# Recurrence levels: only the second blocks' columns, two sets of PSUM banks, and ScalarE copies at the two widest levels

## The chip, the cores and the metric

The kernel runs on one core of one Trainium2 chip. The metric is device time in microseconds (us) of one execution. The engines of the core work side by side, each through its own queue in order: TensorE (matrix products, in the profile PE, with the weight loads apart as PEld), VectorE (DVE), ScalarE (ACT), GpSimd (POOL) and SyncE (SP, which issues transfers). TensorE writes its products to PSUM, and VectorE and ScalarE read them from there; GpSimd works on SBUF alone in this kernel.

## What is computed

The reference is a stack of eight steps on `x` of shape (2, 1024, 256) in float32: an adapter and a recurrent attention, a two-layer net and a mixture of experts, a sparse attention and a local attention, an adapter and a gated feed-forward net. The change lies in the recurrent attention, whose core is this scan over 1024 tokens for each of two sequences and four heads of 64 channels:

```python
def step(S, inputs):
    rt, kt, vt, wt = inputs
    kv = kt[..., :, None] * vt[..., None, :]
    y = jnp.einsum('bhi,bhij->bhj', rt, S + u[None, :, :, None] * kv)
    S = wt[..., :, None] * S + kv
    return (S, y)
```

Unrolled, token t gets from an earlier token s the value v[s], weighted by the sum over channels i of r[t,i] k[s,i] times the decays w[.,i] of all tokens between s and t; and from itself v[t], weighted with u in place of decays. The weights of all pairs (s, t) within a chunk of 128 tokens are what the kernel calls A; what comes from earlier chunks goes through a state of 64 x 64 for each head.

## The kernel before, in words

Channels lie on the 128 partitions, in two groups `c`: partition p of group c is channel 128c + p. A group holds two heads; `par` (0 or 1) says which, so `halves[par]` are the 64 partitions of one head. Tokens run along the free dimension: `r[b]`, `kk[b]` and `w[b]` are tiles of 128 x 2 x 1024 for sequence b. There are NC = 8 chunks of 128 tokens, each in two halves of H = 64 tokens. `A[b]` has the earlier token s on the partitions (two halves of 64) and, for each `par`, `c` and chunk, the later token t along the free dimension.

`wkv` (line 378) fills A by doubling. First the diagonal: `ru` is r times u (line 527, ScalarE), the products of k and ru of all pairs within each half chunk go to PSUM, and VectorE multiplies them with a repeated unit matrix into A (line 528). Then six levels, l = 0 to 5, with h = 2^l. At a level the tokens are seen as pairs of blocks of h tokens. The products of k and r of all pairs within each half chunk are formed again (`scores`, line 410), and of these only the pairs with s in the first and t in the second block of a pair of blocks are kept: VectorE's `copy_predicated` (line 537) copies, under a mask `k.lvl[:, l]`, the columns of the second blocks into A. After that `decay` (from line 420) multiplies k of all first blocks with the total decay of the second block (line 426, GpSimd), r of all second blocks with that of the first (line 427, VectorE), and forms the totals of the doubled blocks (line 429, VectorE). So k and r carry at each level just the decay between blocks that the level needs, and each level of a sequence needs the `decay` of the level before. `last` (line 432) does the step from 64 to 128: the products of each chunk's first half as s with its second half as t, copied to A by ScalarE and VectorE (line 446), with a last `decay`. The levels run for sequence 0 and sequence 1 in turn.

A step of a level has 2 groups x 8 chunks x 2 halves x 2 heads = 128 products. Each takes 64 x 64 weights (64 channels of one head, 64 tokens s) and 64 columns (tokens t). The head chooses the half of the array's rows, the half chunk that of its columns, so four different ones can lie in the array at once.

PSUM: `scores` and `last` use two tiles `sc0` and `sc1`, one per head, of 128 x (2 x 8 x 64) float32, 4 KB per partition each, in a pool with one buffer for each name. So all steps, of both sequences, use the same memory in turn, and the products of one step for a head wait until the copy of the step before has read that head's tile. Another pool (`wkq`, four banks) serves the state and output products.

What sets the order: the program is written as straight code, and the framework's planner places each instruction in its engine's queue by a priority that follows the program's order and by a model of when its operands are ready. It may take ready work ahead: the totals of line 429, which need the decays alone, stand before the levels in VectorE's queue (from 134.9 us), and in the timeline eight output products (line 498) stand at 211.9 us, among the last level's products. On each engine the queue then runs in order. Within a level the written order is: the products of sequence b, the copies of both heads, the multiply of k on GpSimd, the multiply of r on VectorE; then the other sequence.

After the last level, `states` transposes k (line 459), forms the chunk states (line 476) and scans them (line 486), and `output` forms y from A, v, the states and r (lines 498 and 509). The network's further steps follow from y.

Of the kernel before, what the change touches and what calls it, by code (L numbers as in the profile page):

```python
# [9 lines left out]
F32 = mybir.dt.float32  # L10
# [8 lines left out]
P = 128  # L19
# [43 lines left out]
def tiles(tc, **how):  # L63

    return tc.tile_pool(reuse_waits="tile", **how)
# [312 lines left out]
def wkv(k, r, kk, w, v, y, x):  # L378
# [6 lines left out]
    nc, tc = k.nc, k.tc  # L385
    NC = S // P
    M = NC - 1
    H = P // 2
    halves = [slice(i * H, i * H + H) for i in range(2)]
    with (  # L390
# [3 lines left out]
        eye = ap.tile([P, H], F32, name="eye")  # L394
# [3 lines left out]
        A = [ap.tile([P, 2, 2, NC, P], F32, name=f"A{b}") for b in range(B)]  # L398
# [1 line left out]
        for b in range(B):  # L400
            nc.gpsimd.memset(A[b][halves[1], :, :, :, H:P].rearrange("p a c n t -> p (a c n) t"), 0.0)

        def scores(pp, b, rr, take):
            ps = [pp.tile([P, 2, NC, H], F32, name=f"sc{par}") for par in range(2)]
            for c in range(2):
                for ck in range(NC):
                    for half in range(2):
                        ts = slice(ck * P + half * H, ck * P + (half + 1) * H)
                        for par in range(2):
                            nc.tensor.matmul(  # L410
                                ps[par][halves[half], c, ck, :],
                                lhsT=kk[b][halves[par], c, ts],
                                rhs=rr[halves[par], c, ts],
                                start=True,
                                stop=True,
                            )
            for par in range(2):
                take(A[b][:, par, :, :, 0:H].rearrange("p c n t -> p (c n) t"), ps[par].rearrange("p c n t -> p (c n) t"))

        def decay(sp, b, l):  # L420
            h = 1 << l
            n = 2 * S // (2 * h)
            t2 = tot[b].rearrange("p (n two) -> p n two", two=2)
            kv = kk[b].rearrange("p c (n two h) -> p (c n) two h", two=2, h=h)
            rv = r[b].rearrange("p c (n two h) -> p (c n) two h", two=2, h=h)
            nc.gpsimd.tensor_mul(kv[:, :, 0, :], kv[:, :, 0, :], t2[:, :, 1].unsqueeze(2).to_broadcast([P, n, h]))
            nc.vector.tensor_mul(rv[:, :, 1, :], rv[:, :, 1, :], t2[:, :, 0].unsqueeze(2).to_broadcast([P, n, h]))
            nt = sp.tile([P, n], F32, name=f"tot{l}", bufs=2)
            nc.vector.tensor_mul(nt, t2[:, :, 0], t2[:, :, 1])
            tot[b] = nt  # L430

        def last(pp, b):

            ps = [pp.tile([P, 2, NC, H], F32, name=f"sc{par}") for par in range(2)]
            for c in range(2):
                for ck in range(NC):
                    for par in range(2):
                        nc.tensor.matmul(
                            ps[par][halves[0], c, ck, :],
                            lhsT=kk[b][halves[par], c, ck * P : ck * P + H],  # L440
                            rhs=r[b][halves[par], c, ck * P + H : (ck + 1) * P],
                            start=True,
                            stop=True,
                        )
            for par, copy in enumerate((nc.scalar.copy, nc.vector.tensor_copy)):
                copy(
                    A[b][halves[0], par, :, :, H:P].rearrange("p c n t -> p (c n) t"),
                    ps[par][halves[0]].rearrange("p c n t -> p (c n) t"),
                )
            decay(ap, b, 6)  # L450

        def states(sp, b):
# [70 lines left out]
        with tiles(tc, name="wks", bufs=2) as sp, tiles(tc, name="wkp", bufs=1, space=PSUM) as pp:  # L523
            for b in range(B):
                ru = sp.tile([P, 2, S], F32, name="ru")
                for c in range(2):
                    nc.scalar.activation(ru[:, c, :], r[b][:, c, :], AF.Copy, scale=k.vec("u", c))
                scores(pp, b, ru, lambda d, ps: nc.vector.tensor_mul(d, ps, eye.unsqueeze(1).to_broadcast([P, 2 * NC, H])))
            for l in range(6):
                h = 1 << l  # L530
                for b in range(B):

                    def take(d, ps):

                        dv, pv = (t.rearrange("p g (n two h) -> p g n two h", two=2, h=h)[:, :, :, 1, :] for t in (d, ps))
                        m = k.lvl[:, l].rearrange("p g (n h) -> p g n h", h=h)
                        nc.vector.copy_predicated(dv, m, pv)

                    scores(pp, b, r[b], take)
                    decay(sp, b, l)  # L540
            for b in range(B):
                last(pp, b)
# [1160 lines left out]
def program(ctx: ExitStack, tc: tile.TileContext, ins, out):  # L1703
# [16 lines left out]
    with tiles(tc, name="w0", bufs=1) as wp:  # L1720
        load_adapter0(k, wp)
        with tiles(tc, name="rkwv", bufs=1) as ap:
            r, kk, w = ([ap.tile([P, 2, S], F32, name=f"{n}{b}") for b in range(B)] for n in "rkw")
            v = ap.tile([P, NBLK, C], F32, name="v")
            with tiles(tc, name="zero", bufs=1) as zp:
                load_attn0(k, wp, zp)
                load_late(k, lp)
                z = zp.tile([P, ROW], F32, name="z")
                nc.vector.memset(z, 0.0)
                for t, n in ((xs, 2 * NSLOT), (ys, 2 * T)):  # L1730
                    f = t.shape[-1]
                    for i in range(n // 1024):
                        nc.sync.dma_start(
                            out=t[i * 1024 : (i + 1) * 1024, :].rearrange("(p j) f -> p j f", p=P),
                            in_=z[:, 0:f].unsqueeze(1).to_broadcast([P, 8, f]),
                        )
                tmix_in(k, x, r, kk, w, v)
            with tiles(tc, name="y0", bufs=1) as yp:
                y = yp.tile([P, 2, T], F32, name="y")
                wkv(k, r, kk, w, v, y, x)  # L1740
# [139 lines left out]
```

## Time and profile before

| what | us |
|---|---|
| median of 3 runs (lowest, highest) | 1566.27 (1561.85, 1575.56) |
| profiled execution, its own time | 1573.28 |
| its span in the profile | 1571.6 |
| first diagonal product to first product of level 0 | 141.5 to 150.1 |
| the twelve level steps | 150.1 to 213.0 |
| last blocks' products | 213.0 to 222.6 |
| TensorE's products in the levels (1536), busy | 46.5 |
| VectorE's masked copies (24), busy | 20.3 |
| GpSimd's multiplies of k (14), busy | 32.2 |

Lines below such as `L410 PE MATMUL sc<-r,k 64*64 64x64 f32 x1536 | busy us, mean ns | idle` read: line of the program, engine, operation, tile written and tiles read, the part of the array used (rows*columns), partitions x elements, and the count; then the sum of their times, the mean of one, and the engine's idle time just before them with what ended it. In the timeline, a row begins with its start and the length of the merged stretch in us. In the table by stretches, each engine's busy time is followed by its count of instructions, then come the granted share of TensorE's full clock, the share of the transfer engines, and GB/s. TensorE's products are pipelined: a product's own duration contains its way through the array, and what it costs is the distance from start to start. "issue" is idle time that ended with no wait for another engine in the records.

### The profile page before, as it was taken

The numbers are of one execution on the slowest core, as the hardware profiler recorded it, in microseconds if no ns is written. First come the engines' busy times: TensorE is split into PE (matmuls) and PEld (weight loads), VectorE is DVE, ScalarE is ACT, GpSimd is POOL, SyncE is SP. The second block draws the span as 40 slices with busy tenths as digits, with TensorE's granted clock in tenths as the row PEclk, the third lists the DMA queues.
The fourth block names the chain that finished last, engine by engine and source line by source line (L and its number), as shares of the span: only waits on it lengthen the run. The fifth ranks groups of instructions, "written<-read, shape, count | busy, mean of one in ns | idle before, by whom it ended". The sixth has DMA issues, their size and how long they took to land. (4 is left out here: it accounts for less than half of the span.)

```text
span 1571.6 us, 27458 instructions
## 1 busy us (share of the span) xinstructions
PE 1453.8 (93%) x10842; PEld 994.2 (63%) x10842; DVE 876.0 (56%) x2791; ACT 686.1 (44%) x1675; POOL 186.6 (12%) x167
## 2 busy tenths in 40 slices
PE   5998779999869999979999989999999999999897
PEld 2445768544646676655666634778886478888765
DVE  3544663599931111055888711788782167878454
ACT  2433013333421212204988821667574265656543
POOL 1532430014411011010000010000000000000021
PEclk8899678999979999987999999999999999999999
DMA  9500003401153333030000020000000000000001
GB/s 301 176 1 2 3 3 112 161 4 40 53 162 132 124 115 115 14 120 1 2 2 2 2 82 0 1 2 2 1 2 1 0 1 2 2 1 2 1 19 36
DMA packets 42631, 70.79 MB, mean 45 GB/s; under 512 B 7040, under 2 KB 35712, under 8 KB 39424
## 3 DMA queue, kind: packets, MB, share of 16 engines
q1 hardware_dynamic: 36224, 56.11, 10.7%
q0 software_dynamic: 3072, 8.65, 1.5%
q10 hardware_dynamic: 3200, 4.19, 0.8%
q8 instruction: 88, 1.44, 0.4%
q14 instruction: 47, 0.39, 0.1%
HBM read 45.09 MB, written 23.86 MB: 44 GB/s over the span
## 5 line engine op out<-in xcount | busy, mean ns | idle before, releaser
L1543 ACT ACTIVATE pe<-pe,nm 128x320 f32<-128x320 f32 x256 | 141.9, 555 | 133.3 <-DVE nm L1533 133.1
L1533 DVE CUSTOM_DVE_ANT_0 pe<-ps,wbs 128x320 f32<-128x320 f32 x256 | 118.7, 487 | 5.9 <-PE ps L1527 2.5
L1174 ACT ACTIVATE pe<-pe,nm 128x256 f32<-128x256 f32 x256 | 110.6, 498 | 22.1 <-DVE nm L1164 22.1
L942 PE MATMUL ph<-xt,w 128*128 128x512 f32 x256 | 114.2, 604 | 2.0 <-ACT xt L937 2.0
L1523 PE MATMUL ps<-kT,qT 64*128 64x384 f32 (+1 forms) x512 | 109.2, 498 | 3.3 <-DVE qT L1497 2.8
L950 PE MATMUL po<-w,h 128*128 128x256 f32 x512 | 111.8, 379 | 0.0
L950 PEld LDWEIGHTS po<-w,h 128*128 128x128 f32 x512 | 97.3, 190 | 16.6 <-issue 3.8
L1164 DVE CUSTOM_DVE_ANT_0 pe<-ps,lc 128x256 f32<-128x256 f32 x256 | 94.0, 417 | 19.7 <-PE ps L1148 19.7
L953 DVE TENSOR_TENSOR ye<-po,b 128x256 f32<-128x256 f32 x32 | 13.6, 425 | 163.8 <-PE po L950 163.8
L881 DVE SCALAR_TENSOR_TENSOR lc<-iok,idx,lc 128x256 f32<-128x256 f32 x248 | 103.7, 476 | 0.0
L1592 PE MATMUL py<-ptt,v 128*64 128x128 f32 x1408 | 102.3, 277 | 0.1
L942 PEld LDWEIGHTS ph<-xt,w 128*128 128x128 f32 x256 | 48.6, 193 | 62.2 <-issue 55.8
L1592 PEld LDWEIGHTS py<-ptt,v 128*64 128x64 f32 x1408 | 78.2, 137 | 10.5 <-issue 7.6
L1183 PE MATMUL ptp<-ident,pe 128*128 128x128 f32 x512 | 76.8, 291 | 5.8 <-ACT pe L1174 3.2
L1565 PE MATMUL pt<-ident,pe 128*128 128x128 f32 x512 | 79.0, 281 | 1.8 <-DVE pe L1551 0.7
L1183 PEld LDWEIGHTS ptp<-ident,pe 128*128 128x128 f32 x512 | 57.6, 146 | 35.6 <-ACT pe L1174 21.2
L945 ACT ACTIVATE h<-ph,vecs 128x512 f32<-128x512 f32 x64 | 44.0, 687 | 70.7 <-PE ph L942 70.7
L1552 ACT ACTIVATE pe<-pe,rd 128x320 f32<-128x320 f32 x128 | 70.7, 558 | 5.7 <-DVE rd L1550 5.6
L1527 PEld LDWEIGHTS ps<-sk,qT 64*128 64x128 f32 x512 | 50.7, 187 | 26.0
L1427 PE MATMUL pq<-c,w1ak 128*128 128x512 f32 x128 | 61.3, 623 | 5.6 <-ACTq L1765 5.6
L1572 DVE TENSOR_TENSOR ptt<-pt,tri 128x512 f32<-128x512 f32 x96 | 64.9, 676 | 0.0
L1565 PEld LDWEIGHTS pt<-ident,pe 128*128 128x128 f32 x512 | 56.2, 141 | 9.9 <-ACT pe L1552 1.3
(339 smaller groups left out, 2828.2 us busy)
## 6 DMA issues: line engine op xcount, KB each, us to landing
w<-in_mw SPq DMA_DIRECT2D x16, 1024.0 KB, 5.0
xs<-z SPq DMA_DIRECT2D x8, 1088.0 KB, 11.7
xe<-xs SPq DMA_DIRECT2D x8, 544.0 KB, 6.0
more<-xs SPq DMA_DIRECT2D x8, 544.0 KB, 4.0
ys<-z SPq DMA_DIRECT2D x4, 1024.0 KB, 11.4
x<-in_xT ACTq DMA_DIRECT2D x4, 512.0 KB, 5.8
g<-ys SPq DMA_DIRECT2D x4, 512.0 KB, 9.6
g<-ys ACTq DMA_DIRECT2D x4, 512.0 KB, 10.9
```

The lines of the kernel that those rows point to most:

```text
L881: nc.vector.scalar_tensor_tensor(n, key, k.idx[:, qb, j : j + 1], n, ALU.is_equal, ALU.add)
L942: nc.tensor.matmul(ph, lhsT=w1[:, c, m * P : (m + 1) * P], rhs=xt[:, c, :], start=c == 0, stop=c == 1)
L950: nc.tensor.matmul(po, lhsT=h[:, m, j * P : (j + 1) * P], rhs=w2[:, m, :], start=m == 0, stop=m == 7)
L1164: nc.vector.tensor_tensor_reduce(out=pe[:, j, :], in0=it["ps"][i][:, j, :], in1=k.lc[:, q0 + j, :], scale=-1.0, scalar=3.0e38, op0=ALU.add ...
L1174: nc.scalar.activation(pe[:, j, :], pe[:, j, :], AF.Exp, bias=nm, scale=-1.0)
L1183: nc.tensor.transpose(ptp[:, kb, j, :], it["pe"][i][:, j, kb * P : (kb + 1) * P], k.ident)
L1523: nc.tensor.matmul(ps[:, i, keys[i]], lhsT=qs[i], rhs=kT[hp, m + pair, k0 : k0 + nk], start=True, stop=True)
L1533: nc.vector.tensor_tensor_reduce(out=pe[:, i], in0=ps[:, i, used[i]], in1=wbs[:, 0 if n == 0 else 3 if n == NB - 1 else 1 + i, (1 - i) * G ...
L1543: nc.scalar.activation(pe[:, i], pe[:, i], AF.Exp, bias=nm[:, i : i + 1], scale=-1.0, accum_out=den[:, i : i + 1])
L1552: nc.scalar.activation(pe[:, 1], pe[:, 1], AF.Copy, scale=rd[:, 1:2])
L1565: nc.tensor.transpose(pt[1 - j if i and inner(n) else j][:, 2 * pair + i, :], pe[:, at : at + P], k.ident)
L1592: nc.tensor.matmul(py[64 * i : 64 * i + 64, (m + pair) % 4, :], lhsT=keys[:, hs], rhs=it["pts"][:, pair, :] if j == 3 else it["pt"][:, j, ...
```

## The change

`scores` becomes two functions. `diagonal` forms the same diagonal products, but with one tile of 2 KB per partition for each group c and head, and a VectorE multiply after each group (four of 512 elements for each sequence, before two of 1024). `level` gives the products only the columns of the second blocks, h of every 2h tokens: 32 columns for 64, read from r in runs of h, and written without gaps into one tile of 2 KB per head. All these tiles have one name with four buffers, so that two steps' products have different memory. For h below 16 the masked copy stays, now reading dense columns. For h = 16 and 32 there is no mask: the parts of the tile that belong to a pair of blocks are copied one by one by ScalarE, for h = 16 four pieces of 16 partitions x 256 for each head, and for h = 32 two pieces of 32 partitions x 512. `last` takes a tile per group and head and copies after each group. The loads, `decay`, the order of the calls and everything outside `wkv` are as before.

```diff
@@ -400,22 +400,58 @@
         for b in range(B):
             nc.gpsimd.memset(A[b][halves[1], :, :, :, H:P].rearrange("p a c n t -> p (a c n) t"), 0.0)
 
-        def scores(pp, b, rr, take):
-            ps = [pp.tile([P, 2, NC, H], F32, name=f"sc{par}") for par in range(2)]
+        def bank(pp, shape):
+            return pp.tile(shape, F32, name="sc", bufs=4)
+
+        def diagonal(pp, b, ru):
+
+            for c in range(2):
+                ps = [bank(pp, [P, NC, H]) for par in range(2)]
+                for ck in range(NC):
+                    for half in range(2):
+                        ts = slice(ck * P + half * H, ck * P + (half + 1) * H)
+                        for par in range(2):
+                            nc.tensor.matmul(
+                                ps[par][halves[half], ck, :],
+                                lhsT=kk[b][halves[par], c, ts],
+                                rhs=ru[halves[par], c, ts],
+                                start=True,
+                                stop=True,
+                            )
+                for par in range(2):
+                    nc.vector.tensor_mul(A[b][:, par, c, :, 0:H], ps[par], eye.unsqueeze(1).to_broadcast([P, NC, H]))
+
+        def level(pp, b, l):
+
+            h = 1 << l
+            ps = [bank(pp, [P, 2, NC, H // 2]) for par in range(2)]
             for c in range(2):
                 for ck in range(NC):
                     for half in range(2):
                         ts = slice(ck * P + half * H, ck * P + (half + 1) * H)
                         for par in range(2):
+                            rv = r[b][halves[par], c, ts].rearrange("p (n two h) -> p n two h", two=2, h=h)
                             nc.tensor.matmul(
                                 ps[par][halves[half], c, ck, :],
                                 lhsT=kk[b][halves[par], c, ts],
-                                rhs=rr[halves[par], c, ts],
+                                rhs=rv[:, :, 1, :],
                                 start=True,
                                 stop=True,
                             )
             for par in range(2):
-                take(A[b][:, par, :, :, 0:H].rearrange("p c n t -> p (c n) t"), ps[par].rearrange("p c n t -> p (c n) t"))
+                dv = A[b][:, par, :, :, 0:H].rearrange("p c n t -> p (c n) t")
+                dv = dv.rearrange("p g (n two h) -> p g n two h", two=2, h=h)[:, :, :, 1, :]
+                pv = ps[par].rearrange("p c n t -> p (c n) t").rearrange("p g (n h) -> p g n h", h=h)
+                if h < 16:
+                    m = k.lvl[:, l].rearrange("p g (n h) -> p g n h", h=h)
+                    nc.vector.copy_predicated(dv, m, pv)
+                    continue
+
+                for s0 in range(0, P, 32):
+                    n = (s0 % H) // (2 * h)
+                    if s0 % (2 * h) < h:
+                        ss = slice(s0, s0 + min(h, 32))
+                        nc.scalar.copy(dv[ss, :, n, :], pv[ss, :, n, :])
 
         def decay(sp, b, l):
             h = 1 << l
@@ -431,22 +467,19 @@
 
         def last(pp, b):
 
-            ps = [pp.tile([P, 2, NC, H], F32, name=f"sc{par}") for par in range(2)]
             for c in range(2):
+                ps = [bank(pp, [P, NC, H]) for par in range(2)]
                 for ck in range(NC):
                     for par in range(2):
                         nc.tensor.matmul(
-                            ps[par][halves[0], c, ck, :],
+                            ps[par][halves[0], ck, :],
                             lhsT=kk[b][halves[par], c, ck * P : ck * P + H],
                             rhs=r[b][halves[par], c, ck * P + H : (ck + 1) * P],
                             start=True,
                             stop=True,
                         )
-            for par, copy in enumerate((nc.scalar.copy, nc.vector.tensor_copy)):
-                copy(
-                    A[b][halves[0], par, :, :, H:P].rearrange("p c n t -> p (c n) t"),
-                    ps[par][halves[0]].rearrange("p c n t -> p (c n) t"),
-                )
+                for par, copy in enumerate((nc.scalar.copy, nc.vector.tensor_copy)):
+                    copy(A[b][halves[0], par, c, :, H:P], ps[par][halves[0]])
             decay(ap, b, 6)
 
         def states(sp, b):
@@ -525,18 +558,10 @@
                 ru = sp.tile([P, 2, S], F32, name="ru")
                 for c in range(2):
                     nc.scalar.activation(ru[:, c, :], r[b][:, c, :], AF.Copy, scale=k.vec("u", c))
-                scores(pp, b, ru, lambda d, ps: nc.vector.tensor_mul(d, ps, eye.unsqueeze(1).to_broadcast([P, 2 * NC, H])))
+                diagonal(pp, b, ru)
             for l in range(6):
-                h = 1 << l
                 for b in range(B):
-
-                    def take(d, ps):
-
-                        dv, pv = (t.rearrange("p g (n two h) -> p g n two h", two=2, h=h)[:, :, :, 1, :] for t in (d, ps))
-                        m = k.lvl[:, l].rearrange("p g (n h) -> p g n h", h=h)
-                        nc.vector.copy_predicated(dv, m, pv)
-
-                    scores(pp, b, r[b], take)
+                    level(pp, b, l)
                     decay(sp, b, l)
             for b in range(B):
                 last(pp, b)
```

## The prediction

> **What bounds the kernel now.** I read the page first (shares and the 40 slices), then the groups of 140 to 223 us, the timeline of one level, the table by stretches, and the records of the instruction queue.
>
> From the page:
>
> ```profile
> span 1571.6 us, 27458 instructions
> PE 1453.8 (93%) x10842; PEld 994.2 (63%) x10842; DVE 876.0 (56%) x2791; ACT 686.1 (44%) x1675; POOL 186.6 (12%) x167
> PEclk8899678999979999987999999999999999999999
> ```
>
> TensorE is the busy engine over all, but slices 5 and 6 (157 to 236 us) hold the recurrence, where it is granted 0.6 to 0.7 of its clock. The edit touches 141 to 223 us alone. Groups of 140 to 223 us (busy, mean ns | idle before, and what ended it):
>
> ```profile
> L410 PE MATMUL sc<-r,k 64*64 64x64 f32 x1536 | 46.5, 272 | 16.9 <-DVE A L537 12.0 <-issue 3.5 <-DVE A L528 1.3
> L426 POOL TENSOR_TENSOR k<-k,tot 128x1024 f32<-128x1024 f32 x12 | 26.6, 2219 | 35.1 <-PE sc L410 29.5 <-PE sc L438 3.5 <-issue 2.2
> L427 DVE TENSOR_TENSOR r<-r,tot 128x1024 f32<-128x1024 f32 x11 | 21.9, 1990 | 0.0
> L537 DVE COPY_PREDICATED A<-lvls,sc 128x512 f32<-128x512 uint8 x24 | 20.3, 912 | 22.9 <-PE sc L410 22.8
> L528 DVE TENSOR_TENSOR A<-sc,eye 128x1024 f32<-128x1024 f32 x4 | 4.7, 1220 | 4.3 <-PE sc L410 4.3
> ```
>
> TensorE waits for VectorE's copies (12.0 us) and VectorE for TensorE's products (22.8 us): they take turns. ScalarE does nothing from 145 to 217 us. One step (level 1, first sequence) in the timeline:
>
> ```profile
> 162.42 4.76 PE L410 MATMUL sc<-r,k 64*64 64x64 f32 x128 [1.51 <-DVE A L537]
> 167.24 2.44 DVE L537 COPY_PREDICATED A<-lvls,sc 128x512 f32<-128x512 uint8 x2 [2.22 <-PE sc L410]
> 167.38 2.39 POOL L426 TENSOR_TENSOR k<-k,tot 128x1024 f32<-128x1024 f32 x1 [3.45 <-PE sc L410]
> 168.68 4.73 PE L410 MATMUL sc<-r,k 64*64 64x64 f32 x128 [1.49 <-DVE A L537]
> 169.48 1.37 DVE L427 TENSOR_TENSOR r<-r,tot 128x1024 f32<-128x1024 f32 x1
> ```
>
> Products 4.8 us, then TensorE stands until the first copy has emptied a bank: the other sequence's products need nothing but banks. Twelve such steps run from 150.09 to 213.01: 62.9 us, 5.24 each. By stretches (columns: us, busy by engine, granted clock, DMA):
>
> ```profile
> 162.40:174.90 12.50, 9.50 (x257) 9.20 (x257) 7.68 (x7) 0.00 (x0) 5.22 (x3) 0.50 0.01 3
> 183.70:193.10 9.40, 6.80 (x256) 6.38 (x256) 6.55 (x7) 0.00 (x0) 4.10 (x3) 0.82 0.01 3
> 213.00:223.00 10.00, 9.05 (x130) 8.78 (x131) 6.72 (x5) 1.53 (x2) 4.36 (x3) 0.50 0.01 3
> ```
>
> No engine is full in the first two.
>
> **The change, part by part.** The profiled execution took 1573.28 us (span 1571.6 and 1.7 around it), 0.45% above the median 1566.27. Savings are summed in its trace and taken off the median.
>
> *32 columns for 64.* The 128 products of a step stay 128, each with its weight load of 64 columns. In steady flow four of them (one per quarter of the array) start every 58 ns at full clock and every 107 ns at half. Is that the columns or the loads? The nearest row has 128-column weights and products of 2 columns:
>
> ```profile
> 248.40 1.95 PE L577 MATMUL nv<-sel,nsq 128*128 128x2 f32 x16
> ```
>
> (1.95 - 0.25) / 15 = 113 ns each, and the transposes of 128 columns with as many weights come every 109. So the load binds: 64 columns of weights cost some 56 ns (full clock) whether 64 or 32 columns follow, and this edit saves TensorE nothing. Other end: time in proportion to columns, half. I take the row. The Trainium skill, TensorE: Matmul & The Clock Gate (Back-to-back issue gap), speaks against the edit for another reason: some 25 ns from start to start for any product of 1 to 64 columns. That floor would make 128 x 25 = 3.2 us a step even at full clock; the diagonal's 128 products, at full clock, start 58 / 4 = 15 ns apart and are through in 2.20 us, so I sum with the trace.
>
> A step of products then takes 128 x 107 / 4 = 3.41 us at half clock, 1.87 at full. Today's 4.8 hold more: the first 32 or so go two by two, one row half alone (starts 107 ns apart per pair), because its bank is emptied first. With free banks that order goes.
>
> The clock: the same page of the Trainium skill (What's actually happening) has it open after about 3.4 us of activity. By that, gapless products would run at full clock. The row 213 to 223 speaks against: busy 9.05 of 10.00 us with half of the quarters in use, and 0.50 all along. Products of half the columns use the array about as little, so I take half clock (3.41); the rule would give 1.87 and leave the step to the next two bounds.
>
> *Two sets of banks.* A step's products no longer wait for the copies of the step before. Next late: the r of the same sequence (VectorE's copies, then its multiply) and k (GpSimd, 2.0 to 2.8 us). VectorE's work per step: level 0 2.49 + 1.76 = 4.25; level 1 2.44 + 1.37, with gaps 3.9; levels 2 and 3 1.30 + 2.1 = 3.4; levels 4 and 5 2.0. The copies read dense from PSUM now, where they took every second run: 1.24 us each at levels 0 and 1, 0.65 above. I keep the 1.24, since the written side stays as cut up; dense they might be 0.65 (2.4 us less over four steps).
>
> *Instruction supply.* "issue" ended 20.4 us of TensorE's two rows' idle time in the level products (21 times). The instruction queue's records show why: one 16 KB packet per 256 records of TensorE (one step), and in the fast steps the last 8 or 10 products start 2.35 to 2.7 us after such a packet (packet 184.69, products 187.05). Successive packets at 184.69, 189.39, 194.12 and 198.75 are 4.7 us apart, with bank waits within; once (146.11, 149.49) 3.4. So a step costs at least 3.4, and 4.7 if that spacing is its own. I take 3.8, nearer to 3.4, since about 0.9 of each 4.7 is the wait that the banks take away.
>
> *ScalarE's copies.* Level 4: eight of 16 x 256 per sequence; the row "half<-py", 128x256 from PSUM, took 0.375: 3.0 us. Level 5: four of 32 x 512 at 0.59 (kt<-pk): 2.35. They replace 1.30 of VectorE, on an engine idle there; behind them nothing is queued before the last blocks' copies. Only the products of the step after next wait for them (the same set of banks), and 3.0 < 3.8: nothing. Without that cover +1.7 us a step at level 4 and +1.0 at level 5.
>
> *Diagonal and last.* Eight multiplies of 512 for four of 1024: (1.22 x 4 = 4.9) becomes about 8 x 0.69 = 5.5, but the first starts after half the products and frees banks 1.3 us earlier. The second sequence's last products still wait for the packet (146.11 today, about 145 then): level 0 starts at about 147.5 instead of 150.09: -2.6. The last blocks: 213.01 to 222.64 = 9.6 us; 2 x 64 x 107 / 2 = 6.8 with no bank wait between, and a supply stall and the tail: 7.9, -1.7. The smaller copies there lie under the products of the other half; uncovered, about 0.3 for each of the eight.
>
> Sum of the levels: 8.5 + 7.8 + 8 x 3.8 = 46.7 for 62.9: **-16.2**. With -2.6 and -1.7: **-20.5**. What follows (states, output) starts from the last products and the decays, as now, and the rest hangs on that; nothing independent of it fills 141 to 223. 1566.27 - 20.5 = 1545.8.
>
> **The rivals.**
> 1. *Likeliest (0.56):* as above, 1545.8; by the unknowns 1541 to 1551.
> 2. *Supply binds (0.20):* 4.65 us a step: 12 x 4.65 = 55.8, -7.1; diagonal and last as above: -11, 1555. For it: three spacings of 4.6 to 4.7 in a row. Against: each of those holds a bank wait of about 0.9, and the one of 3.4.
> 3. *The narrow products count (0.16):* full clock or half the array time, and dense copies: VectorE and supply at 3.4 to 3.5: 12 x 3.45 = 41.4, -21.5, -3, -2.5: -27, 1539. For it: nothing in the trace has 64 weights and 32 columns. Against: the 113 ns.
> 4. *No overlap (0.04):* the planner queues VectorE so that the next products still come after it: the wait of 1.0 to 1.5 moves from the bank to r. Left: the two-by-two start (0.85 a step) partly, and the ends: about -6, 1560.
> 5. *Gapped reads, slower (0.04):* the moving operand is now read in runs of h with gaps of h, from single elements at level 0. Price: above 12 x 5.6 us (62.9 + 4.3 saved elsewhere) it is a loss, that is 175 ns per four or 5.5 ns per column, against 1.67 in sequence at half clock. At 7 ns: 224 ns, 7.2 us a step, 86 us; +23 - 4.3: 1585. The nearest row reads weights in steps of 28 bytes (py<-r,st): its loads take 208 ns for 133 in sequence at full clock, so 0.83 + 75 / 64 = 2.0 ns per column: 64 ns for 32, under the load's 107. Even that worst stride hides.
>
> **How the numbers follow.** Case 1 straddles the bound of 1% (15.7 us, about what a measurement of this kernel can tell from no change) with some 15% of its weight below it. Faster: 0.56 x 0.85 + 0.16 + a little of case 2 = 0.66; same 0.29; slower 0.05. The range runs from case 3 with the spread of three runs' medians (1537) to case 2 with the same (1558).
>
> **What would show it.** Right: L410's successor in rows of 64x32 with about the same busy time, its waits for "A" gone; level stretch about 47 us; PEclk near 0.5 there; copies of A on ScalarE of about 0.37 and 0.59; "issue" as the largest idle of TensorE. Wrong: products in less than 3 us at half clock (case 3), packets 4.6 apart without waits (case 2), means of a step's products above 5 us (case 5). The forecast fails most easily by the supply, which no view prices alone.

## The result and the profile after

The changed kernel takes 1549.01 us (median of 4 runs, 1543.76 to 1552.1), the kernel before beside it 1570.91 (4 runs, 1561.85 to 1575.7): ratio 0.9875, 95% interval 0.9841 to 0.991. That is 1.25% less (by the interval 0.9 to 1.6%); the forecast was 1545.8, 1.31% less. The profiled execution of the changed kernel took 1550.45 us, its span 1548.7.

The same lines of the page of the changed kernel:

```profile
span 1548.7 us, 27485 instructions
PE 1445.2 (93%) x10842; PEld 987.7 (64%) x10842; DVE 864.8 (56%) x2789; ACT 696.2 (45%) x1701; POOL 194.8 (13%) x167
PEclk9799579999799999987999999999999999999999
```

The count of TensorE's instructions is the same and its busy time 8.6 us shorter. The levels now lie mostly in the fifth slice of the clock's row (155 to 194 us), and the clock is as low there as before: 5, where it was 6.

Since the recurrence began anywhere from 140.1 to 146.6 us in the different profiles, I compare stretches from the first diagonal product. The first transposition of k after the last blocks (row "pk<-ident,k") begins 81.03 us after it in the profile of before and 60.82 us in that of after: 20.2 us earlier, where the prediction had 20.5. The two spans differ by 22.9. The recurrence of after began 0.5 us later, so 3.2 us came in behind it, where the program is the same; the runs of one kernel spread by more than that.

The groups of 135 to 215 us of the changed kernel (busy us, mean ns | idle before, and what ended it):

```profile
L434 PE MATMUL sc<-r,k 64*64 64x32 f32 x1536 | 41.8, 280 | 5.5 <-issue 4.4 <-DVE r L463 0.8 <-DVE A L422 0.2
L462 POOL TENSOR_TENSOR k<-k,tot 128x1024 f32<-128x1024 f32 x12 | 31.7, 2642 | 16.2 <-PE sc L434 14.8 <-PE sc L474 1.4
L463 DVE TENSOR_TENSOR r<-r,tot 128x1024 f32<-128x1024 f32 x12 | 18.4, 1533 | 8.8 <-PE sc L434 8.8
L447 DVE COPY_PREDICATED A<-lvls,sc 128x512 f32<-128x512 uint8 x16 | 15.2, 1031 | 4.9 <-PE sc L434 4.9
L454 ACT COPY A<-sc 16x256 f32<-16x256 f32 x16 | 5.8, 363 | 38.9 <-PE sc L434 38.7
L422 DVE TENSOR_TENSOR A<-sc,eye 128x512 f32<-128x512 f32 x8 | 5.1, 686 | 1.7 <-PE sc L414 1.7
L454 ACT COPY A<-sc 32x512 f32<-32x512 f32 x8 | 4.6, 575 | 2.8 <-PE sc L434 2.7
```

The 16.9 us that TensorE stood before its level products are 5.5, and "DVE A" (the banks) is down from 13.3 to 0.2; what is left is "issue". The narrow products' busy time is 41.8 for 46.5. Level 1 with the products beside the copies, level 4, and a copy of level 5, in the timeline of the changed kernel:

```profile
155.85 7.27 PE L434 MATMUL sc<-r,k 64*64 64x32 f32 x249 [0.80 <-DVE r L463]
159.75 2.46 DVE L447 COPY_PREDICATED A<-lvls,sc 128x512 f32<-128x512 uint8 x2 [0.27 <-PE sc L434]
159.89 2.41 POOL L462 TENSOR_TENSOR k<-k,tot 128x1024 f32<-128x1024 f32 x1 [1.50 <-PE sc L434]
162.00 1.38 DVE L463 TENSOR_TENSOR r<-r,tot 128x1024 f32<-128x1024 f32 x1
163.33 3.63 PE L434 MATMUL sc<-r,k 64*64 64x32 f32 x127 [0.21 <-issue]
163.80 2.46 DVE L447 COPY_PREDICATED A<-lvls,sc 128x512 f32<-128x512 uint8 x2 [0.42 <-PE sc L434]
...
182.52 3.64 PE L434 MATMUL sc<-r,k 64*64 64x32 f32 x128 [0.19 <-issue]
183.02 3.00 ACT L454 COPY A<-sc 16x256 f32<-16x256 f32 x8 [37.87 <-PE sc L434]
183.09 1.23 DVE L463 TENSOR_TENSOR r<-r,tot 128x1024 f32<-128x1024 f32 x1 [0.65 <-PE sc L434]
183.19 2.94 POOL L462 TENSOR_TENSOR k<-k,tot 128x1024 f32<-128x1024 f32 x1 [1.83 <-PE sc L434]
186.35 3.65 PE L434 MATMUL sc<-r,k 64*64 64x32 f32 x127 [0.19 <-issue]
...
190.83 2.35 ACT L454 COPY A<-sc 32x512 f32<-32x512 f32 x4 [0.98 <-PE sc L434]
```

TensorE no longer takes turns with the copies: it runs on while they read the other set of banks, and goes from step to step with 0.2 us between. From 182.52 to 186.35 a step is 3.83 us, where it was 5.24. By stretches (us, busy PE, PEld, DVE, ACT, POOL, granted clock, DMA):

```profile
163.30:178.70 15.40, 14.64 (x510) 14.18 (x511) 13.61 (x13) 0.00 (x0) 8.63 (x4) 0.50 0.02 4
178.70:194.40 15.70, 14.79 (x517) 14.25 (x520) 6.93 (x6) 8.11 (x20) 10.81 (x4) 0.50 0.02 5
194.40:202.90 8.50, 7.79 (x140) 7.41 (x137) 4.55 (x6) 4.46 (x8) 6.45 (x3) 0.50 0.01 4
```

TensorE is full in the first two (14.64 of 15.40), at half clock in all three. The twelve level steps run from 148.13 to 194.4 us: 46.3 us, where they took 62.9.

### The profile page after: what moved, and what is told of

Its sections match the earlier page's. It is cut to its first block, busy times and chain, and to the rows that moved or that the text cites. A ratio compares the mean times of both kernels' runs of the same rounds, so it can differ in the third digit from the quotient of the medians.

```text
span 1548.7 us, 27485 instructions
## 1 busy us (share of the span) xinstructions
PE 1445.2 (93%) x10842; PEld 987.7 (64%) x10842; DVE 864.8 (56%) x2789; ACT 696.2 (45%) x1701; POOL 194.8 (13%) x167
## 6 DMA issues: line engine op xcount, KB each, us to landing
xs<-z SPq DMA_DIRECT2D x8, 1088.0 KB, 11.5
```

## The experiments

The table sums up twelve kernels; the first two columns are from the profile, in us from the first diagonal product. The whole time of a single run is uncertain by 1% (the kernel before took 1558 to 1576), so kernels with one run are judged by these columns and by their rows.

| kernel | first level product | first transposition of k | whole time (runs) |
|---|---|---|---|
| before | 8.55 | 81.03 | 1570.91 (4) |
| changed | 5.49 | 60.82 | 1549.01 (4) |
| one_set | 11.55 | 100.21 | 1597.12 (4) |
| one_set_cols | 9.58 | 85.58 | 1579.18 (1) |
| wide_groups | 5.44 | 59.51 | 1551.03 (4) |
| all_cols | 5.44 | 58.85 | 1545.61 (1) |
| half_products | 5.76 | 59.74 | 1547.79 (1) |
| few_products | 5.52 | 58.24 | 1541.93 (1) |
| load32 | 5.45 | 60.36 | 1554.45 (1) |
| vector_copies | 5.44 | 60.09 | 1548.26 (4) |
| r_first | 5.77 | 63.22 | 1551.16 (5) |
| eight_products | 5.44 | 51.02 | 1542.43 (1) |

A word on counts: a step has 2 x 8 x 2 x 2 = 64 products in the program, and the profile has two records for each (1536 in twelve steps). The "128 products" of the description and of the prediction are these records. The durations were taken per record, so the sums built on them stand; the one that does not is the 128 x 25 = 3.2 us of the prediction, which is 64 x 25 = 1.6 us if the 25 ns are meant for each product of the program.

**One set of banks.** All else is as in the changed kernel.

```diff
-            return pp.tile(shape, F32, name="sc", bufs=4)
+            return pp.tile(shape, F32, name="sc", bufs=2)
```

> The changed kernel with two buffers for the recurrence's PSUM tiles in place of four: each step's products must again wait for the copies of the step before. Narrow products and ScalarE's copies stay. Theory (the second set of banks carries the gain): TensorE and the copies take turns again, a step is 3.4 us of products and 0.3 of their way out, the first head's copy (1.25 at levels 0 and 1, 0.65 at 2 and 3, 1.5 at 4, 1.2 at 5), and some 0.8 of products that go two by two: levels 58 to 65 us for 46.4, and the whole 12 to 20 us over the changed kernel, close to the kernel before. Rival (the narrow products or the copies' engine carry it): levels below 52 us, at most 6 us over the changed kernel.

1597.12 us beside 1567.2 for the kernel before: ratio 1.0188 (1.0149 to 1.0227), clear of noise slower than before, and 48 us above the changed kernel. From its timeline:

```profile
189.14 4.91 PE L434 MATMUL sc<-r,k 64*64 64x32 f32 x128 [0.89 <-DVE A L447]
213.05 5.97 PE L434 MATMUL sc<-r,k 64*64 64x32 f32 x128 [1.63 <-ACT A L454]
219.06 3.00 ACT L454 COPY A<-sc 16x256 f32<-16x256 f32 x8 [4.60 <-PE sc L434]
```

The wait for "A" is back before eleven of the twelve steps, and the products go two by two again at the start (4.91 us, and 5.97 behind ScalarE's copies, which empty the second head's bank late). The twelve steps take 77 us (157.8 to 234.9). So the second set is what carries the gain. But one set alone should have brought back the kernel before, and it cost 30 us more; the expectation missed that. Of these 30, 19.2 lie in the table's stretch (100.21 for 81.03); the profile of one_set also began the recurrence 4.7 us later (146.2 for 141.5), where the programs are the same, and that part is not explained. Between one_set and the kernel before lie the narrow columns, ScalarE's copies and the smaller tiles of the diagonal and the last blocks, and its clock:

```profile
180.00:200.00 20.00, 16.57 (x450) 16.12 (x446) 10.39 (x10) 0.00 (x0) 6.61 (x3) 0.50 0.01 3
```

0.50 at levels 2 and 3 (and from 150.6 to 256.4 us without a break), where the kernel before had 0.82 in 183.7 to 193.1. Hence the next run.

**One set of banks, all columns.** As one_set, with products of all 64 columns.

```diff
-                                ps[par][halves[half], c, ck, :],
+                                ps[par][halves[half]].rearrange("p c n t -> p (c n t)")[:, ck * H : (ck + 1) * H],
...
-                                rhs=rv[:, :, 1, :],
+                                rhs=r[b][halves[par], c, ts],
```

> One set of banks again, but products of all 64 columns (the second group's columns are written over the first's, so half of the scores in the half chunks are lost). If the narrow products' low clock is what made one set cost 48 us more than two and 30 more than the kernel before, the clock comes back to 0.65 to 1.0 in the levels, a step falls from 6.5 to about 5.2 as in the kernel before, the levels take 60 to 65 us and the time is within 1% of the kernel before's. Rival: something else in the narrow banks with one set costs the 30 (the order of the two banks, the copies by ScalarE): levels of 72 us or more, about 1590.

```profile
181.94 2.60 PE L433 MATMUL sc<-r,k 64*64 64x64 f32 x128 [0.89 <-DVE A L446]
206.89 2.35 ACT L453 COPY A<-sc 32x512 f32<-32x512 f32 x4 [3.78 <-PE sc L433]
208.15 4.82 PE L433 MATMUL sc<-r,k 64*64 64x64 f32 x128 [1.31 <-DVE r L462]
```

```profile
178.70:189.00 10.30, 7.65 (x344) 7.29 (x338) 7.15 (x7) 0.00 (x0) 4.11 (x2) 0.90 0.01 3
```

The clock is back (0.90 here), a step's products fall to 2.6 us where it is open, and the levels take 64.6 us (149.7 to 214.3), as expected. The first transposition comes 14.6 us before one_set's; 2.0 of that lie in the diagonal, which the two kernels have alike, and 12.7 in the levels. It is still 4.5 us behind the kernel before: 1.0 in the diagonal, 1.7 in the levels and 1.9 in the last blocks (11.5 us for 9.6), whose smaller tiles now alternate with the copies in one set. In the levels, the waits for ScalarE's copies at 4 and 5 (1.5 us, where VectorE's cost 0.8 to 0.9 before) may be part of the cause. The time of the single run was 0.9% above the kernel before (1565.11 beside it).

**All columns, two sets.** The same edit with four buffers.

> The changed kernel with 64 columns for 32 in each level product; the second group's products fall on the first's place in the bank, so half of the scores are lost and nothing else differs. Theory (weight loads bind, the clock follows the columns): at half clock four products start every 107 ns as now; with twice the columns the clock opens for part of the levels, a step falls from 3.8 to 3.4 to 3.7, then VectorE (4.25 at levels 0 and 1) and the instruction packets bind: levels 42 to 46 us for 46.4. Rival A (columns count): levels 60 us and more at half clock. Rival B (the clock follows whether products are queued, not their columns): clock 0.50 and 46.4 us as now.

Timeline, and a stretch:

```profile
172.69 2.13 PE L433 MATMUL sc<-r,k 64*64 64x64 f32 x128 [1.71 <-issue]
176.24 2.22 PE L433 MATMUL sc<-r,k 64*64 64x64 f32 x127 [1.43 <-issue]
```

```profile
179.00:194.40 15.40, 8.62 (x437) 7.93 (x438) 6.39 (x6) 10.69 (x25) 11.30 (x4) 1.00 0.02 5
```

At full clock the 64 columns are through in 2.1 to 2.2 us, and then TensorE stands 1.4 to 1.7 us for "issue". The instruction queue's packets come 3.85, 3.84, 3.54, 3.55 and 3.71 us apart from 166.24 to 184.73. TensorE's gaps end with no wait for another engine, lie inside a step and not at its end, and end 2.3 to 2.4 us after a packet begins (173.93 and 176.24, 177.47 and 179.89). So with the loads out of the way the instruction supply holds the step, at just about the 3.83 of the changed kernel at half clock. The first transposition moves by 2.0 us only: the levels are 1.0 us shorter, the last blocks, which the open clock reaches too, 2.4 (5.8 for 8.2), and 1.5 of that is lost again in a longer wait for k.

With the two one-set kernels this makes a square, in us to the first transposition of k:

| | one set | two sets | gain of the second set |
|---|---|---|---|
| 32 columns | 100.21 | 60.82 | 39.4 |
| 64 columns | 85.58 | 58.85 | 26.7 |
| cost of narrowing | 14.6 | 2.0 | |

Narrowing does not pay by itself in either column (each kernel profiled once). What it does is to halve the PSUM that a step needs.

**All columns, computed rightly.** all_cols loses scores; this one keeps them, with a tile per group and head and, since ScalarE would need twice the pieces, VectorE's masked copies at all levels.

```diff
-            ps = [bank(pp, [P, 2, NC, H // 2]) for par in range(2)]
             for c in range(2):
+                ps = [bank(pp, [P, NC, H]) for par in range(2)]
...
-                                rhs=rv[:, :, 1, :],
+                                rhs=r[b][halves[par], c, ts],
...
-                if h < 16:
...
```

> The changed kernel with 64 columns for each product as before, in tiles per group and head as the diagonal has them, four buffers, so that the two groups of a step use different banks; masked copies on VectorE at all levels (48 of 256 elements). Theory (columns cost nothing, overlap is what counts): within 3 us of the changed kernel, 17 to 22 us below the kernel before; VectorE has 1.6 to 2.6 us of copies in a step for 1.3 to 2.5. Rival (narrow products carry it): 10 us or more over the changed kernel.

1551.03 us, ratio 0.9892 (0.9853 to 0.9931): the changed kernel's gain without narrow products and without ScalarE. Timeline and a stretch:

```profile
186.31 2.28 PE L433 MATMUL sc<-r,k 64*64 64x64 f32 x128 [1.47 <-issue]
190.14 2.46 PE L433 MATMUL sc<-r,k 64*64 64x64 f32 x127 [1.55 <-issue]
```

```profile
179.00:194.40 15.40, 9.44 (x513) 8.61 (x508) 15.20 (x20) 0.00 (x0) 8.02 (x4) 1.00 0.02 4
```

Here a step's four tiles are only one set for a whole step, but each group's copies run while the other group's products do. The step is 3.83 us again (186.31 to 190.14), with the full clock, TensorE idle for 1.5 of it, and VectorE full (15.20 of 15.40); which of supply and VectorE would hold it without the other is not separated. The kernel takes no more PSUM than before: four tiles of 2 KB for two of 4. The second set came from filling and emptying the same 8 KB in smaller parts.

**Half the products.** The products of the second half of each chunk are left out, and the copies read the first half's partitions alone.

```diff
-                    for half in range(2):
+                    for half in range(1):
...
```

> The changed kernel with the products of each level's second half chunk left out (64 for 128 a step), copies of the first half's 64 partitions alone and as many of them as now; scores of the second halves stay without the levels' part. What binds when neither products nor instruction packets can: theory: VectorE at levels 0 to 3 (4.2, 3.8, 3.4, 3.4 a step), ScalarE's 3.0 and GpSimd's 2.9 at 4 and 5: levels 41 to 43 us for 46.4. So a step of 3.8 is 3.4 of products and little above the next bound. Rival (a step is held by waits between engines, not by TensorE): levels stay within 1.5 us of 46.4.

```profile
177.96 3.62 PE L434 MATMUL sc<-r,k 64*64 64x32 f32 x64 [0.57 <-POOL k L462]
185.54 2.95 POOL L462 TENSOR_TENSOR k<-k,tot 128x1024 f32<-128x1024 f32 x1 [0.84 <-PE sc L434]
```

This told nothing apart: half the records take the same 3.62 us, because with half the array's columns two start every 107 ns in place of four, at half clock. The levels took 45.7 us (146.3 to 192.0), where 41 to 43 was expected on the assumption that the products would not bind.

**Fewer, larger products.** Both halves' tokens in one product of 128 weights and 128 columns, written over one another.

```diff
+                    ts = slice(ck * P, (ck + 1) * P)
+                    at = min(ck, NC - 2) * H
+                    for par in range(2):
+                        nc.tensor.matmul(
+                            ps[par].rearrange("p c n t -> p (c n t)")[:, at : at + P],
+                            lhsT=kk[b][halves[par], c, ts],
+                            rhs=r[b][halves[par], c, ts],
...
```

> The changed kernel with a quarter of the products in each level step: 32 for 128, each with the 128 tokens of a chunk as weights and 128 columns, so that pairs across half chunks are formed and fall over their neighbours in the bank; the levels' scores are lost, the copies, multiplies and the rest are as they are. TensorE has 64 records a step for 256, and at full clock some 1.8 us of work. Theory (at a step of 3.8 half clock and the instruction packets bind about equally): with both gone, levels 0 and 1 fall only to VectorE's 4.2 and 3.8, levels 2 and 3 to 3.4, levels 4 and 5 to the 3.0 of ScalarE's copies and GpSimd: 40 to 43 us for 46.4. Rival (the waits between engines hold the step, whatever TensorE does): 45 us or more.

```profile
154.29 36.93 PE L433 MATMUL sc<-r,k 64*128 64x128 f32 x640 [0.64 <-DVE r L462]
```

Ten steps without a break, 36.93 / 10 = 3.69 us each, at full clock (1.00 from 142 to 203 us) and with packets 6.8 to 8.1 us apart: the supply is out of the way, but a pair of records starts every 112 ns, 64 x 56 = 3.58 us a step. The expectation missed this. At the same full clock all_cols starts four records every 58 ns: here half as many run side by side, and each takes twice as long. That is 3.58 us for half the records, near the changed kernel's 3.6 at half clock. Weights and columns were both doubled, so this run alone does not say which of the two sets the 112 ns.

**Level 5 with half the weights.** At the last level only the first 32 of each 64 tokens s are needed.

```diff
+                            o = halves[half] if h < 32 else slice(half * H, half * H + 32)
+                            cs = ts if h < 32 else slice(ts.start, ts.start + 32)
...
-                                lhsT=kk[b][halves[par], c, ts],
+                                lhsT=kk[b][halves[par], c, cs],
```

> The changed kernel with the weights of level 5 cut to the 32 tokens of the first block of each half chunk, which are all that this level keeps; its products are still 128 with 32 columns. Theory (the weight load sets the pace): four products start every 54 to 60 ns at half clock for 107, so the products of a step take 1.8 us, and its two steps fall from 3.9 to what instruction packets and GpSimd allow, 3.3 to 3.8 each; the whole gains about 1 us. Rival (another cost per product sets the pace): 107 ns as at the other levels.

```profile
171.34 7.39 PE L436 MATMUL sc<-r,k 64*64 64x32 f32 x255 [0.19 <-issue]
...
190.47 2.06 PE L436 MATMUL sc<-r,k 64*32 64x32 f32 x127 [2.11 <-issue]
194.39 0.43 PE L436 MATMUL sc<-r,k 64*32 64x32 f32 x12 [1.87 <-issue]
```

The rows from 171.34 and 190.47 are at a clock of 0.50. The columns are the same 32; with 32 weights in place of 64 four records start every 53 to 54 ns for 107, and 127 records take 2.06 us for 3.65. (From 186.5 to 189.9 us the clock was open, and there it was 33 ns for 58.) So the weight load sets the pace, at half clock in proportion to the weights. From gap to gap the time is no shorter: 190.47 to 194.39 is 3.92 us, with 1.9 to 2.1 of "issue". Behind the loads stands the supply.

**VectorE's masked copies at levels 4 and 5.**

```diff
-                if h < 16:
+                if h < 64:
```

> The changed kernel with masked copies on VectorE at levels 4 and 5 too, none on ScalarE. Theory: VectorE has 1.3 + 2.0 = 3.3 in a step of 3.8, so nothing is lost: levels 46 to 47 us for 46.4, the whole within 2 us of the changed kernel. Rival (ScalarE's copies carry a part of the gain): 4 us or more over the changed kernel.

1548.26 us, ratio 0.9883 (0.9839 to 0.9927): no difference.

```profile
189.51 7.37 PE L434 MATMUL sc<-r,k 64*64 64x32 f32 x255 [0.46 <-issue]
190.02 1.32 DVE L447 COPY_PREDICATED A<-lvls,sc 128x512 f32<-128x512 uint8 x2 [0.90 <-PE sc L434]
190.28 1.96 POOL L462 TENSOR_TENSOR k<-k,tot 128x1024 f32<-128x1024 f32 x1 [2.24 <-PE sc L434]
191.24 2.08 DVE L463 TENSOR_TENSOR r<-r,tot 128x1024 f32<-128x1024 f32 x1
```

Two masked copies and r are 3.4 us on VectorE, under TensorE's 3.7. ScalarE's copies carry nothing.

**r between the copies.** At each level VectorE copies the first head, then multiplies r, then copies the second head, so that the next level's r is ready earlier.

```diff
+            decay(sp, b, l)
...
-                    level(pp, b, l)
-                    decay(sp, b, l)
+                    level(sp, pp, b, l)
```

> The changed kernel with each level's multiplies of k and r called ahead of its copies; the planner then queues them on VectorE as one copy, r, the other copy. At levels 4 and 5, where r already starts with k, r takes 1.23 and k 2.9, in place of 2.0 and 2.0 when r starts later. Theory: at levels 0 and 1, where VectorE's 4.2 and 3.8 a step are longer than TensorE's work, r comes 1.25 us earlier, and the wait for it goes: 1 to 2 us less in the levels, nothing that three rounds can tell (within 3 us). Rival: GpSimd's multiply, slowed to 2.9 or more, becomes late: levels longer by 1 us or more.

1551.16 us, ratio 0.9911 (0.9872 to 0.995): no gain. The expected 1 to 2 us less in the levels did not come.

```profile
176.60 2.03 POOL L463 TENSOR_TENSOR k<-k,tot 128x1024 f32<-128x1024 f32 x1 [2.48 <-PE sc L434]
177.06 2.66 DVE L464 TENSOR_TENSOR r<-r,tot 128x1024 f32<-128x1024 f32 x1
```

Moved forward, r lies beside GpSimd's k for 1.6 us of its time, for 0.9 in the changed kernel, and takes 2.66 us for 2.0; the first transposition comes 2.4 us later than in the changed kernel.

**Eight products a step.** The last question is what is left if loads and supply both go.

```diff
-                for ck in range(NC):
-                    for half in range(2):
-                        ts = slice(ck * P + half * H, ck * P + (half + 1) * H)
+                for half in range(2):
+                    ts = slice(half * (S // 2), (half + 1) * (S // 2))
...
-                                lhsT=kk[b][halves[par], c, ts],
+                            lhsT=kk[b][halves[par], c, half * H : (half + 1) * H],
```

> Each level step has eight products of 256 columns with the weights of one chunk, in place of 128 of 32 columns: almost no loads and no instructions, and everything behind them as in the changed kernel. (Scores are wrong within the half chunks: the products of the chunks after the first are formed with the first one's weights.) It shows what VectorE and GpSimd alone allow. If TensorE's loads and the instruction supply together hold the step at 3.8, as my theory says, the step falls to what the vector side costs: 4.2 and 3.9 at levels 0 and 1 as before, 3.4 at levels 2 and 3 (copies 1.3, multiply of r 2.1), 2.9 at levels 4 and 5 (GpSimd's multiply of k): 41.5 us for 46.3, about 1542 to 1545. Rival: the vector side is what holds the step, and loads and supply only fill its time: levels of 45 to 46 us, no change.

```profile
177.61 1.99 PE L433 MATMUL sc<-r,k 64*64 64x256 f32 x16 [0.95 <-DVE r L462]
178.59 13.36 DVE L462 TENSOR_TENSOR r<-r,tot 128x1024 f32<-128x1024 f32 x5
180.55 1.98 PE L433 MATMUL sc<-r,k 64*64 64x256 f32 x16 [0.96 <-DVE r L462]
```

```profile
163.30:178.70 15.40, 9.46 (x81) 4.34 (x80) 15.40 (x17) 0.00 (x0) 14.15 (x6) 0.50 0.00 1
```

The levels take 37.2 us (152.0 to 189.2), and the first transposition comes 9.8 us before the changed kernel's. TensorE now waits for r, and VectorE is full (15.40 of 15.40). So loads and supply do hold the changed kernel's step, and not the vector side. My 41.5 for the vector side was too high: the two steps of level 0 take 6.0 us together (expected 8.4), those of level 1 3.4 to 3.8 each, those of levels 2 to 5 2.9 to 3.4, though at levels 4 and 5 r and k slow each other (five multiplies of r in 13.36 us, 2.67 each).

## Why the prediction was right

*Two sets of banks.* Right, and the whole of the gain in the levels: 46.3 us where the sum said 46.7. One_set loses it, and wide_groups has it without narrow products and without ScalarE. That the sum is so close is in part luck. Level by level it said 8.5 (level 0), 7.8 (level 1) and 30.4; measured were 7.7, 7.7 and 30.9. Level 0 was not held by VectorE's 4.25 a step, as it had it: TensorE waited 1.2 and 1.4 us there for "issue" and 0.8 for r.

*32 columns for 64: nothing saved, since the load binds.* Right. Four records start every 107 ns at half clock with 32 columns as with 64, and load32 halves that by halving the weights alone. At full clock it is 58 ns with 32 columns (level 0 of the changed kernel) and 58 with 64 (all_cols). The two-by-two start did go: at half clock a step's products take 3.6 us, for 4.8. Of this TensorE's busy time shows 4.7 us in the twelve steps, since the kernel before had the full clock for part of levels 2 to 5 (0.78 to 0.83 on average) and the changed one did not. Rival 3, that narrow products count, is out, and so is rival 5: from level 1 on the 107 ns are the same at every level, whatever the length of the runs that r is read in. Rival 4, no overlap, is answered by the rows of level 1 and 4 above.

*The clock: half.* Right for the changed kernel (0.50 without a break from 155 to 203 us), and it speaks against the rule of the Trainium skill weighed there (TensorE: Matmul & The Clock Gate, What's actually happening): TensorE was busy for 14.64 of 15.40 us, and the clock did not open in 48. The same page's 25 ns from start to start is no floor between records here: all_cols has 128 of them in 2.13 us, about 17 ns each. For each product of the program that is 33 ns, above the 25, so the prediction's use of it against the edit rests on its count. What the prediction did not see is the other half of this step: with 64 columns in two sets the clock is open, so narrowing has a price. It hardly shows in the time, since the supply takes what the clock gives.

*Instruction supply, 3.8 a step.* Right in size: steps of 3.83 us at level 4, packets 3.55 to 3.98 apart from 165 us on. Rival 2 (4.65) is out. But the prediction named one bound where there are two of the same height: at half clock the loads (3.6 and a stall of 0.2), at full clock the supply (all_cols, 3.54 to 3.85). That the two came out alike is luck for the sum. Taking one away leaves the other, which is why all_cols, load32 and few_products, each of which removes one, hardly move, and eight_products, which removes both, gains 9.8 us.

*ScalarE's copies, 3.0 and 2.35, hidden.* Right: 3.00 and 2.35 measured, and vector_copies shows that they are worth nothing either way.

*Diagonal and last, -2.6 and -1.7.* The bulk of level 0's products started 6.05 us after the first diagonal product for 8.55, -2.5; the last blocks took 8.2 us for 9.6, -1.4. The copies at levels 0 and 1 stayed at 1.23 to 1.26 us each though they read dense, as taken.

*The total.* -20.5 forecast; -20.2 to the first transposition of k, -21.9 between the medians (from the interval of the ratio: 14 to 25 us). That the time is 1549.0 and not 1545.8 is the level of before, which was 1570.9 in four runs, where the forecast started from 1566.27.

The expectations failed in five places behind it: one_set's extra cost (12.7 us of it the lower clock of narrow products, by one_set_cols), half_products and few_products (both still bound by TensorE's products; the 113 ns of the prediction's own row, 128 weights with 2 columns, could have told the second), r_first, and the vector side in eight_products (41.5 for 37.2).

Why the clock stays low is open. Narrow products do not shut it for good: it opened for 3.4 us in load32 (186.5 to 189.9) and for 6.8 in r_first (170.8 to 177.6). Nor does it take narrow ones: eight_products, with 256 columns in each, had 0.50 from 157.8 us on. What these two kinds share is the number of columns in a step, 128 x 32 = 16 x 256, where all_cols and wide_groups have twice as many; but eight_products also leaves TensorE idle, so that is no test. Whether a packet's spacing of 3.6 us is the queue's or the sequencer's stays open too, and so does a version better than both kernels: load32 computes all scores with fewer weights to load and gains nothing, and no run computes them with fewer records.

## What to carry to other kernels

When two engines take turns over PSUM, look first for room for a second set of banks: here it was worth 27 us with wide products and 39 with narrow ones (20 against the kernel before, which was the faster with one set). The narrowing that made room saved TensorE no time, and wide_groups shows that smaller tiles make the same room. Before making products smaller, find whether the columns or the weight loads set the distance from start to start, and look at the granted clock after. When one bound is removed and nothing moves, suspect a second one of the same height: take away both at once.

## What the runs showed of the hardware

- Behind loads of 64 weights, four records of 64 x 64 start every 107 ns at half clock and every 58 ns at full, with 32 columns as with 64. With 32 columns the clock stayed at 0.50 for 48 us of almost gapless work (after); with 64 and two sets it was 0.89 to 1.00 (all_cols, wide_groups).
- Instruction supply can hold small products: in all_cols the packets for 128 records and their loads come every 3.54 to 3.85 us, 14 to 15 ns for each of the 256, and TensorE stands idle for 1.4 to 1.7 us of it.
- GpSimd and VectorE slow each other when they multiply in SBUF at the same time. In the changed kernel's levels 4 and 5, where r starts 0.1 us first, r takes 1.23 us and k 2.94. At levels 2 and 3, where k starts first, each takes 2.0 to 2.1; r takes 2.4 to 2.7 in r_first, where they lie side by side longer. That the first to start goes ahead is no rule, though: in the changed kernel's last blocks k starts 0.5 us before r, and r takes 1.21, k 3.49.
